# The short tile of tokens moved to the front, the last norm's shift added earlier, the last unit's sums turned on TensorE

## Chip, core and metric

The kernel runs on one core of one Trainium2 chip. The metric is the time on the device in microseconds (us), the median of several runs. A core has five engines with their own instruction streams: TensorE (PE: matrix products and transposes; its weight loads are PEld), VectorE (DVE), ScalarE (ACT), GpSimd (POOL) and SyncE (SP). SP, ACT and POOL also issue transfers (DMA).

## What is computed

800 tokens of 512 elements (8 sequences of 100) go through two layers, each an attention to a context of 8 x 722 rows and a mixture of 8 experts of which each token takes 2, with a residual after each of the four blocks:

```python
x = x + _L0_xattn_ref(_layernorm(x), ctx, ...)  # 16 heads of 32, causal: only the first 100 context rows count
x = x + _L0_ffn_ref(_layernorm(x), ...)         # 8 experts, 512 -> 2048 (GELU) -> 512, softmax weights of the top 2
x = x + _L1_xattn_ref(_layernorm(x), ctx, ...)  # 16 heads of 64; keys and values: own 100 tokens, 722 context rows
x = x + _L1_ffn_ref(_layernorm(x), ...)         # 8 experts, silu(gate) * up, 512 -> 1024 -> 512
```

The last block ends with a norm of its own output, before the residual:

```python
out = jnp.sum(rw[..., None] * sel, axis=2)      # the two experts' answers, weighted
mu, var = mean(out), mean((out - mu) ** 2)
out = (out - mu) * jax.lax.rsqrt(var + LN_EPS)
return out * ln_gamma + ln_beta
```

All is in float32.

## The kernel before

The 800 tokens lie in `x` as 7 tiles of up to 128 rows (one row to a partition): six of 128 and, last, one of 32 (`rows`). Everything that belongs to tokens and not to experts goes tile by tile.

**Layer 0.** After the norm, the columns and the attention, the output phase walks through the tiles (loop in the stage around L606 to L632): output product (L622), residual (L623), norm, transposes (`to_columns`, L153 to L166), router logits (`router_logits`, L173 to L178). Between them TensorE does context products (L425, L437) for attention 1 that are kept in memory.

**Routing.** `Route.group` takes a few tiles together, by the list `GROUPS`: for layer 0 tiles 0-2, 3-4 and 5-6. On VectorE it finds the two largest logits of each token (L227 to L241), marks them (`sel`, L245/L247), sums marks of earlier tiles (`before`, L249); TensorE counts the rows ahead (L252, L253, `ps_rank`); VectorE makes the place in the table (`row`, `pick`, `place`, `where`, L255 to L261); then POOL issues one indirect DMA for each tile and each of the two choices (L267), which scatters normed token rows into the table `sent`. When the last group is placed, `order` (L274 to L311) sorts the experts by their number of tokens; SP and POOL read the order into registers. `arrived` (L338 to L346) gathers an expert's rows from `sent` (L344, `xg`) and transposes them.

**Expert layers.** `work_off` goes through the 8 experts: `hidden0`/`hidden1`, then `products` (L348 to L365) and `returned` (L368 to L377), which writes rows to the table `answers`. `work_off` issues the next expert's `arrived` after the hidden products of the present one, and calls `midway`, if it has one, in the fifth. Layer 0 uses that for `fetch_context`. Weights come in 1 MB tiles on SP's queue (L58), eight buffers, each behind a one-element copy where it must wait (L56).

**Between the layers** each tile's two answers are gathered (`fetch`, L333), weighted and added to `x` (L723), normed and transposed (L724 to L728), and `bo` is added on POOL (L729).

**Attention 1** runs 64 units (8 sequences `b` times 8 pairs of heads `ic`) in a software pipeline: keys and scores of a unit (L778), the largest score (DVE, L782), the exponentials (ACT, L784, with their sums), and, one unit later, the transposes of the weights (L807 to L813), the values (L828) and the division by the sums. In sequences 0 and 1 (`EARLY`), whose keys were projected before, the reciprocal sums are copied wide by POOL (L792), transposed by TensorE (L822) and multiplied in at once (L832, L833). In the others they go to memory by SP (L795) and come back spread over partitions (L797), and the unit is multiplied by `over` a unit later (L835).

The list `due` puts three steps of each tile into the stream of units: `output` (L871 to L881: 16 matmuls L876 with the tile's rows as the stationary side, residual L879, norm) in unit `n`, `logits1` in `n + 1`, `sent_on` (the routing, by GROUPS 0-1, 2-3, 4, 5-6) in `n + 2`. `n` is two units after the last unit of the last sequence that the tile touches: 18, 26, 34, 50 and 58 for tiles 0 to 4. Tiles 5 and 6 both end in sequence 7, so theirs come after the last unit. The order of the instructions on each engine is set by a scheduler from the program.

**Expert layer 1 and the tail.** `gain` and `bias` (ln_gamma and ln_beta, spread over 128 partitions, 256 KB each) are loaded on ACT's queue at the stage's beginning (L929, L931). After the experts the two answers of each tile are gathered (L333), weighted into `acc` (L988, L990), normed, multiplied by `gain` (L998), added to `x` (L999) and stored (L1000). `x + bias` is written in the loop of the tail (L996), on POOL; the scheduler put these seven additions at the entry of the expert layer, where `bias` lands.

Of the kernel before, what the change touches and what calls it, by code (L numbers as in the profile page):

```python
# [8 lines left out]
F32 = mybir.dt.float32  # L9
AF = mybir.ActivationFunctionType  # L10
ALU = mybir.AluOpType
AX = mybir.AxisListType

P = 128
D = 512
DC = D // P
B, T, S = 8, 100, 722
NT = B * T
# [19 lines left out]
ROWS = NE * NT  # L38
GROUPS = ((0, 3), (3, 5), (5, NTILE)), ((0, 2), (2, 4), (4, 5), (5, NTILE))
LAST = NT - NT // P * P  # L40

# [25 lines left out]
def two_layers(ctx: ExitStack, tc: tile.TileContext, a: dict, out: bass.AP):  # L67
    nc = tc.nc
    x_in = a["x"].rearrange("b t d -> (b t) d")
    y_out = out.rearrange("b t d -> (b t) d")  # L70
    rows = [min(P, NT - i * P) for i in range(NTILE)]

# [28 lines left out]
    x = const.tile([P, NTILE, D], F32, name="x")  # L101
    nc.vector.memset(x[:, NTILE - 1, :], 0.0)
    for i0, i1 in ((0, 1), (1, 3), (3, NTILE - 1)):
        nc.scalar.dma_start(out=x[:, i0:i1, :], in_=x_in[i0 * P : i1 * P].rearrange("(i p) d -> p i d", p=P))
    nc.scalar.dma_start(out=x[:LAST, NTILE - 1, :], in_=x_in[NT - LAST :])

# [98 lines left out]
    class Route:  # L205


        def __init__(self, layer, psum, tag):
            self.layer, self.psum, self.tag = layer, psum, tag
            self.logits = routes.tile([P, NTILE, NE], F32, tag="logits", name=f"logits{layer}")  # L210
            nc.vector.memset(self.logits, 0.0)
            self.m = [routes.tile([P, NTILE], F32, tag=f"m{k}", name=f"m{k}_{layer}") for k in range(2)]
            self.where = [
                routes.tile([P, NTILE], mybir.dt.int32, tag=f"where{k}", name=f"where{k}_{layer}") for k in range(2)
            ]
            self.sel = routes.tile([P, NTILE, NE], F32, tag="sel", name=f"sel{layer}")
            nc.vector.memset(self.sel[:, NTILE - 1, :], 0.0)
            self.before = routes.tile([P, NTILE + 1, NE], F32, tag="before", name=f"before{layer}")
            nc.vector.memset(self.before[:, 0, :], 0.0)
# [16 lines left out]
        def group(self, i0, i1, xn):  # L236
# [5 lines left out]
            at2 = self.largest(other, self.m[1][:, i0:i1], 2)  # L242
            full = g if i1 < NTILE else g - 1
            if full:
                nc.vector.tensor_tensor(self.sel[:, i0 : i0 + full, :], at1[:, :full], at2[:, :full], ALU.add)  # L245
            if full < g:
                nc.vector.tensor_tensor(self.sel[:LAST, i1 - 1, :], at1[:LAST, full], at2[:LAST, full], ALU.add)  # L247
            for i in range(i0, i1):
# [221 lines left out]
    with tc.tile_pool(name="a0", bufs=1) as ap, tc.tile_pool(name="a0w", bufs=3) as aw, tc.tile_pool(  # L470
# [91 lines left out]
        for i in range(NTILE):  # L562
            xn = aw.tile([P, D], F32, tag="xn", name="xn0")
            scaled(xn, x[:, i, :], *factors(moments(x[:, i, :], "a0"), "a"))
            to_columns(xT, xn, i * P, rows[i], ps)
            nc.gpsimd.tensor_tensor(x[:, i, :], x[:, i, :], o_b, ALU.add)
# [41 lines left out]
        def logits0(i):  # L608
            xT = xTf[:, :, i * P : i * P + rows[i]]
            to_columns(xT, xl[:, i, :], 0, rows[i], ps)  # L610
            router_logits(route.logits, i, xT, wg0, bg0, ps, "av")
            for i0, i1 in GROUPS[0]:
                if i1 == i + 1:
                    route.group(i0, i1, lambda i: xl[:, i, :])

        for i in range(NTILE):
            w, t0 = rows[i], i * P
            if i % 4 == 0:
# [40 lines left out]
    with f0, tc.tile_pool(name="f0w", bufs=2) as fw, tc.tile_pool(  # L659
# [57 lines left out]
        for i in range(NTILE):  # L717
            w = rows[i]
            both = fp.tile([P, 2, D], F32, tag="nil", name="back0", bufs=2)
            for k, m in enumerate((m1, m2)):  # L720
                y = both[:, k]
                fetch(y, where, i, k)
                nc.vector.scalar_tensor_tensor(  # L723
                    x[:w, i, :], y[:w], m[:w, i : i + 1], x[:w, i, :], ALU.mult, ALU.add  # L724
                )
            xn = fp.tile([P, D], F32, tag="mv", name="xn1", bufs=2)
            scaled(xn, x[:, i, :], *factors(moments(x[:, i, :], "a1"), "b", twice=True))
            to_columns(xT1, xn, i * P, rows[i], ps, gamma1, beta1)  # L728
            nc.gpsimd.tensor_tensor(x[:, i, :], x[:, i, :], bo, ALU.add)  # L729
# [4 lines left out]
    with tc.tile_pool(name="a1", bufs=1) as ap, ExitStack() as later, tc.tile_pool(  # L734
# [25 lines left out]
        def values(b, ic, mT):  # L760
# [5 lines left out]
            return mv  # L766

        def weighed(b, ic, kT, mT):

# [19 lines left out]
            nc.vector.reciprocal(sums, sums)  # L789
            if b < len(EARLY):  # L790
                over = aw.tile([T, 2, H1], F32, tag="share", name="wide1", bufs=4)
                nc.gpsimd.tensor_copy(over, sums.unsqueeze(2).to_broadcast([T, 2, H1]))  # L792
                return prs, over
# [23 lines left out]
        def attended(b, ic, v, mv, prT, over):  # L817


            po = ps.tile([P, 2, T], F32, tag="tp", name="ps_av1")  # L820
            if b < len(EARLY):
                nc.tensor.transpose(po[:, 1, :], over.rearrange("t j d -> t (j d)"), ident[:T, :T])  # L822
# [6 lines left out]
            mine = qT[:, ic, b * T : (b + 1) * T]  # L829
            if b < len(EARLY):  # L830
                wide = small.tile([P, T], F32, tag="over", name="over2")
# [39 lines left out]
        def output(i):  # L871

            w, t0 = rows[i], i * P
            po = ps.tile([P, D], F32, tag="tp", name="ps_o1")
# [21 lines left out]
        for i in range(NTILE):  # L896
            n = min(t0 + T for t0 in range(0, NT, T) if t0 + T >= i * P + rows[i]) // T * IC + 2
            for k, step in enumerate((output, logits1, sent_on)):
# [19 lines left out]
        divide()  # L918
        attended(*before[:4], *turned(*before[4]))()
        for step, i in due[len(units)]:  # L920
# [4 lines left out]
    with tc.tile_pool(name="f1", bufs=1) as fp, tc.tile_pool(name="f1w", bufs=2) as fw, tc.tile_pool(  # L925
        name="f1p", bufs=2, space=bass.MemoryType.PSUM
    ) as ps:
        gain = fp.tile([P, D], F32, name="gain")
        nc.scalar.dma_start(out=gain, in_=a["ln_gamma"].partition_broadcast(P))  # L929
        bias = fp.tile([P, D], F32, name="bias")  # L930
        nc.scalar.dma_start(out=bias, in_=a["ln_beta"].partition_broadcast(P))  # L931
        where, more, (m1, m2) = route.where, route.more, route.m
# [27 lines left out]

        def work1(jobs, first=None):
            work_off(
                jobs, lambda e, r0, n: arrived(1, e, r0, n, fw, ps), hidden1,
                lambda e, n, h, wd: products(n, h, [wd(g) for g in range(NF // 4)], NF, fw, ps),
                lambda e, r0, n, yT: returned(1, e, r0, n, yT, fw, ps), first,
            )
# [6 lines left out]
            for e in range(NE)  # L973
        ], W_L1F)
        rest(
# [4 lines left out]
        acc = fp.tile([P, NTILE, D], F32, name="acc")  # L980
        nc.vector.memset(acc[:, NTILE - 1, :], 0.0)
        for i in range(NTILE):
# [11 lines left out]
        for i in range(NTILE):  # L994
            w = rows[i]
            nc.gpsimd.tensor_tensor(x[:, i, :], x[:, i, :], bias, ALU.add)  # L996
            scaled(acc[:, i, :], acc[:, i, :], *factors(moments(acc[:, i, :], "out"), "a"))
            nc.vector.tensor_tensor(acc[:, i, :], acc[:, i, :], gain, ALU.mult)  # L998
            nc.vector.tensor_tensor(x[:, i, :], x[:, i, :], acc[:, i, :], ALU.add)  # L999
            nc.sync.dma_start(out=y_out[i * P : i * P + w], in_=x[:w, i, :])  # L1000

# [69 lines left out]
```

## Time and profile before

| | us |
|---|---|
| median of 3 runs | 1884.36 |
| lowest and highest | 1884.31, 1885.33 |
| profiled execution, its own time | 1883.63 |
| its span, from the first to the last instruction | 1882.0 |
| PE busy in it | 1725.5 (92%) |
| DVE, ACT, POOL busy | 594.9, 479.7, 147.8 |

The stages in that execution, from the timeline: layer 0's output phase and routing lie about 179 to 231, its expert layer starts with the first transposes at 239.8, attention 1 with L414 at 684.4; the units' stream ends with the last scores near 1482, expert layer 1 starts at 1541.5 and the gathers of the tail at 1845.9.

In the lines of the timeline the columns are the start, the duration, the engine, the line, the operation, output and inputs with their shapes, the count, and in brackets the engine's idle time before it and what ended it. In lines of windows they are the stretch, its length, the busy time of PE, PEld, DVE, ACT and POOL with the number of instructions, the granted clock of TensorE as a share of full speed, the share of the DMA engines, and GB/s.

### The profile page before, as it was taken

To read this page: it belongs to the slowest core of one execution; us is meant where nothing else is said; L and a number is where in the kernel's file an instruction comes from. 1 tells how busy PE (TensorE), PEld (TensorE's weight loads), DVE (VectorE), ACT (ScalarE), POOL (GpSimd) and SP (SyncE) were. 2 spreads that over 40 slices of the span, in tenths; PEclk is the share of its full clock that TensorE was granted. 3 is DMA by queue.
4 is the path that set the end of the run, shared out by engine and by line. 5 is a ranking of instruction groups with operands and counts; after the bars stand their busy time and mean duration, and the time that the engine had idled before them with its cause. 6 is when DMAs were issued, how large, how long until landed. Compare 5 with 4: busy or idle time off the path is not lost. (4 is left out here: it accounts for less than half of the span.)

```text
span 1882.0 us, 26422 instructions
## 1 busy us (share of the span) xinstructions
PE 1725.5 (92%) x10414; PEld 1306.4 (69%) x10414; DVE 594.9 (32%) x1462; ACT 479.7 (25%) x1400; POOL 147.8 (8%) x237
## 2 busy tenths in 40 slices
PE   5999689999999879999999999999999849999990
PEld 2455479999999645666666666666666528999990
DVE  4464510011111220454344424444444331111115
ACT  2364211111111132333333323333333210010110
POOL 4010310000000220000000000000000030000003
PEclk9999889999999989999999999999999969999995
DMA  9901374465555361131020300202201145555523
GB/s 367 414 28 56 124 284 169 182 222 189 203 201 219 108 235 45 40 96 56 5 37 5 59 3 5 37 6 37 27 6 15 6 159 221 192 185 200 207 79 114
DMA packets 74657, 227.87 MB, mean 121 GB/s; under 512 B 26273, under 2 KB 37161, under 8 KB 58129
## 3 DMA queue, kind: packets, MB, share of 16 engines
q1 hardware_dynamic: 53020, 177.98, 27.7%
q0 software_dynamic: 9888, 30.06, 5.1%
q10 hardware_dynamic: 11604, 17.95, 3.2%
q8 instruction: 86, 1.41, 0.3%
q14 instruction: 59, 0.48, 0.1%
HBM read 177.12 MB, written 48.83 MB: 120 GB/s over the span
## 5 line engine op out<-in xcount | busy, mean ns | idle before, releaser
L425 PE MATMUL ps_m<-cb,w 128*128 128x361 f32 x944 | 315.7, 486 | 0.0
L356 PE MATMUL ps_y<-h,w 128*128 128x256 f32 (+7 forms) x1536 | 280.5, 344 | 0.0
L356 PEld LDWEIGHTS ps_y<-h,w 128*128 128x128 f32 x1536 | 268.6, 190 | 7.9
L425 PEld LDWEIGHTS ps_m<-cb,w 128*128 128x128 f32 x944 | 180.5, 196 | 110.5 <-issue 18.0
L680 PE MATMUL ps_h<-xgT,w 128*128 128x256 f32 (+7 forms) x1024 | 189.5, 346 | 0.0
L680 PEld LDWEIGHTS ps_h<-xgT,w 128*128 128x128 f32 x1024 | 180.8, 192 | 5.8
L784 ACT ACTIVATE pr<-ps_sc,m 100x822 f32<-100x822 f32 x128 | 119.9, 942 | 175.7 <-issue 89.9
L808 DVE COPY prT<-ps_ptA 128x500 f32<-128x500 f32 x128 | 82.1, 678 | 187.1 <-PE ps_ptA L807 187.1
L782 DVE TENSOR_REDUCE m<-ps_sc 100x1 f32<-100x822 f32 x128 | 123.8, 1009 | 46.7 <-PE ps_sc L778 46.7
L684 ACT ACTIVATE h<-ps_h,s_b 128x256 f32<-128x256 f32 (+7 forms) x128 | 56.1, 438 | 303.8 <-PE ps_h L680 303.8
L429 ACT COPY mT<-ps_m 128x361 f32<-128x361 f32 x128 | 58.8, 460 | 251.5 <-PE ps_m L425 226.1
L414 PE MATMUL ps_col<-xT,w 128*128 128x400 f32 x320 | 115.1, 518 | 1.3 <-ACT xT L166 1.3
L950 PE MATMUL ps_g<-xgT,w 128*128 128x256 f32 (+7 forms) x512 | 104.3, 347 | 0.0
L950 PE MATMUL ps_u<-xgT,w 128*128 128x256 f32 (+7 forms) x512 | 102.8, 344 | 0.0
L414 PEld LDWEIGHTS ps_col<-xT,w 128*128 128x128 f32 x320 | 61.9, 197 | 47.3 <-issue 4.2
L950 PEld LDWEIGHTS ps_g<-xgT,w 128*128 128x128 f32 x512 | 91.4, 192 | 3.0
L950 PEld LDWEIGHTS ps_u<-xgT,w 128*128 128x128 f32 x512 | 90.7, 190 | 2.7
L778 PE MATMUL ps_sc<-mT,qT 64*100 64x311 f32 (+1 forms) x512 | 91.3, 468 | 0.0
L828 PEld LDWEIGHTS ps_av<-prT,mv 128*64 128x64 f32 (+1 forms) x1536 | 67.9, 137 | 31.3 <-issue 28.9
L955 ACT ACTIVATE sg<-ps_g 128x256 f32<-128x256 f32 (+7 forms) x64 | 22.3, 348 | 238.8 <-PE ps_g L950 238.8
L828 PE MATMUL ps_av<-prT,mv 128*64 128x100 f32 (+1 forms) x1536 | 80.6, 253 | 0.0
L807 PEld LDWEIGHTS ps_ptA<-ident,pr 100*128 100x128 f32 x640 | 65.2, 141 | 20.7 <-issue 10.6
(242 smaller groups left out, 1799.6 us busy)
## 6 DMA issues: line engine op xcount, KB each, us to landing
w<-in_W SPq DMA_DIRECT2D x64, 1024.0 KB
w<-in_w_gate SPq DMA_DIRECT2D x16, 1024.0 KB
w<-in_w_up SPq DMA_DIRECT2D x16, 1024.0 KB
w<-in_w_down SPq DMA_DIRECT2D x16, 1024.0 KB
sent<-nil SPq DMA_DIRECT2D x25, 512.0 KB
answers<-nil SPq DMA_DIRECT2D x25, 512.0 KB
cb<-in_ctxT ACTq DMA_DIRECT2D x16, 722.0 KB
xg<-sent POOLq DMA_DIRECT2D x18, 256.0 KB
```

The costliest lines, as they stand in the source:

```text
L356: nc.tensor.matmul(py[:, k, :n], ws[f // 4][:, f % 4, dc * P : (dc + 1) * P], h[:, f, :n], start=f == 0, stop=f == nf - 1,)
L414: nc.tensor.matmul(ps[:, :HALF], w[c // 4][:, dc, (c % 4) * P : (c % 4 + 1) * P], xT[:, dc, cols], start=dc == 0, stop=dc == DC - 1,)
L425: nc.tensor.matmul(pm[:, : S // 2], w_m[ic // 4][:, dc, (ic % 4) * P : (ic % 4 + 1) * P], cb[h][:, dc, : S // 2], start=dc == 0, stop=dc = ...
L429: nc.scalar.copy(mT[:, h * (S // 2) : (h + 1) * (S // 2)], pm[:, : S // 2])
L680: nc.tensor.matmul(ph[:, :n], w[:, dc, j * P : (j + 1) * P], xg[:, dc, :n], start=dc == 0, stop=dc == DC - 1,)
L778: nc.tensor.matmul(sc[:, bank, c0:c1], qT[r, ic, q0 : q0 + T], keys_, start=True, stop=True)
L782: nc.vector.tensor_reduce(m, sc[:, :, :NKH], AX.XY, ALU.max, negate=True)
L784: nc.scalar.activation(pr.rearrange("p (a n) -> p a n", a=2), sc[:, :, :NKH], AF.Exp, bias=m, accum_out=sums[:, j : j + 1],)
L807: nc.tensor.transpose(pt[:, c, :], pr[:, T + c * P : T + (c + 1) * P], ident[:T, :T])
L808: nc.vector.tensor_copy(prT[:, : NSC - 1, :], pt)
L828: nc.tensor.matmul(po[r, 0, :], vj, prT[j][:w, c, :], start=c == 0, stop=c == NSC)
L950: nc.tensor.matmul(p_[:, :n], w_[:, dc, j * P : (j + 1) * P], xg[:, dc, :n], start=dc == 0, stop=dc == DC - 1,)
```

## The change

Three edits.

- The short tile becomes tile 0 (tokens 0 to 31); tiles 1 to 6 have 128 rows each and start at 32, 160, 288, 416, 544 and 672 (`starts`). `GROUPS` becomes 0-2, 3-5, 6 for layer 0 and 0-1, 2-3, 4-5, 6 for layer 1. By the rule of `due` the tiles' steps now start in units 10 (the short one), 18, 26, 42, 50 and 58, and only tile 6 is left for the end.
- `gain` and `bias` are loaded by `fetch_gains`, which `work_off` calls as `midway` in the fifth expert of layer 1: two one-element copies on POOL that wait for an `xg`, two DMAs on POOL's queue, and the seven additions `x + bias` on POOL. The additions of the tail's loop are gone. In POOL's order they stand after the gather of the sixth expert and before the answers of the third.
- The last unit (sequence 7, heads pair 7) turns its reciprocal sums like the early ones: POOL copies them wide, TensorE transposes them, ACT copies the result out of the accumulators, and VectorE multiplies. Its three transfers by SP are gone.

```diff
-GROUPS = ((0, 3), (3, 5), (5, NTILE)), ((0, 2), (2, 4), (4, 5), (5, NTILE))
-LAST = NT - NT // P * P
+GROUPS = ((0, 3), (3, 6), (6, NTILE)), ((0, 2), (2, 4), (4, 6), (6, NTILE))
+SHORT = NT - NT // P * P
...
-    rows = [min(P, NT - i * P) for i in range(NTILE)]
+    rows = [SHORT] + [P] * (NTILE - 1)
+    starts = [0] + list(range(SHORT, NT, P))
...
-    nc.vector.memset(x[:, NTILE - 1, :], 0.0)
-    for i0, i1 in ((0, 1), (1, 3), (3, NTILE - 1)):
-        nc.scalar.dma_start(out=x[:, i0:i1, :], in_=x_in[i0 * P : i1 * P].rearrange("(i p) d -> p i d", p=P))
-    nc.scalar.dma_start(out=x[:LAST, NTILE - 1, :], in_=x_in[NT - LAST :])
+    nc.vector.memset(x[:, 0, :], 0.0)
+    nc.scalar.dma_start(out=x[:SHORT, 0, :], in_=x_in[:SHORT])
+    for i0, i1 in ((1, 2), (2, 4), (4, NTILE)):
+        of_tiles = x_in[starts[i0] : starts[i0] + (i1 - i0) * P]
+        nc.scalar.dma_start(out=x[:, i0:i1, :], in_=of_tiles.rearrange("(i p) d -> p i d", p=P))
...
+        def turned_here(b, ic):
+
+            return b < len(EARLY) or (b, ic) == (B - 1, IC - 1)
...
-            if b < len(EARLY):
+            if turned_here(b, ic):
                 over = aw.tile([T, 2, H1], F32, tag="share", name="wide1", bufs=4)
                 nc.gpsimd.tensor_copy(over, sums.unsqueeze(2).to_broadcast([T, 2, H1]))
...
-            n = min(t0 + T for t0 in range(0, NT, T) if t0 + T >= i * P + rows[i]) // T * IC + 2
+            n = min(t0 + T for t0 in range(0, NT, T) if t0 + T >= starts[i] + rows[i]) // T * IC + 2
...
-        attended(*before[:4], *turned(*before[4]))()
+        attended(*before[:4], *turned(*before[4]))
...
-        gain = fp.tile([P, D], F32, name="gain")
-        nc.scalar.dma_start(out=gain, in_=a["ln_gamma"].partition_broadcast(P))
-        bias = fp.tile([P, D], F32, name="bias")
-        nc.scalar.dma_start(out=bias, in_=a["ln_beta"].partition_broadcast(P))
+        gain, bias = (fp.tile([P, D], F32, name=n) for n in ("gain", "bias"))
+
+        def fetch_gains(behind):
+
+            for t, n in ((gain, "ln_gamma"), (bias, "ln_beta")):
+                nc.gpsimd.tensor_copy(t[:1, :1], behind[:1, 0, :1])
+                nc.gpsimd.dma_start(out=t, in_=a[n].partition_broadcast(P))
+            for i in range(NTILE):
+                nc.gpsimd.tensor_tensor(x[:, i, :], x[:, i, :], bias, ALU.add)
...
         for i in range(NTILE):
             w = rows[i]
-            nc.gpsimd.tensor_tensor(x[:, i, :], x[:, i, :], bias, ALU.add)
             scaled(acc[:, i, :], acc[:, i, :], *factors(moments(acc[:, i, :], "out"), "a"))
```

The same turns of index (`starts[i]` for `i * P`, tile 0 for the last one) stand in the transposes, the clears of `sel` and `acc`, and the stores.

## The prediction

> **What bounds the kernel now.** I read the page first, then the waits of TensorE, then the timeline of the four places that the change touches: the routing of layer 0, the unit stream of attention 1, the entry of expert layer 1, and the tail.
>
> ```profile
> PE 1725.5 (92%) x10414; PEld 1306.4 (69%) x10414; DVE 594.9 (32%) x1462; ACT 479.7 (25%) x1400; POOL 147.8 (8%) x237
> PEclk9999889999999989999999999999999969999995
> ```
>
> TensorE is busy in 92% of the span, with its dips at the start, near 180 to 240, 660 to 690 and 1490 to 1545, and at the end. So TensorE work that is added inside a stream costs its full length, and other engines cost something only in the dips.
>
> ```profile
> PE ps_tp L157 <- DMA xg<-sent: 29.9, 3, 14.9
> PE ps_sc L778 <- ACT pr L784: 10.3, 10, 1.6
> PE ps_rank L252 <- DVE before L249: 10.2, 2, 9.1
> PE ps_o L876 <- DVE qT L835: 1.3, 1, 1.3
> ```
>
> The columns are total wait, times and longest. The first line is the two entries of the expert layers, the second is two short stalls in each of five output steps, the third is the routing at the end of attention 1, and the last is all that TensorE waits for the last unit's sums.
>
> The entry of expert layer 1, in the timeline (start, length, engine, line, and in brackets the idle time before it):
>
> ```profile
> 1503.59 8.64 PE L876 MATMUL ps_o<-w,qT 128*32 128x512 f32 x16
> 1503.69 0.17 DVE L178 COPY logits<-ps_lg 128x8 f32<-128x8 f32 x1 [3.81 <-PE ps_lg L173]
> 1516.43 8.57 POOL L996 TENSOR_TENSOR x<-x,bias 128x512 f32<-128x512 f32 x7 [59.14 <-DMA bias<-in_ln_beta]
> 1516.86 0.15 DVE L178 COPY logits<-ps_lg 32x8 f32<-32x8 f32 x1 [1.30 <-PE ps_lg L173]
> 1517.75 1.19 DVE L230 TENSOR_TENSOR at<-at,rank 128x16 f32<-128x16 f32 x1
> 1528.11 0.99 POOL L267 DMA_INDIRECT sent<-xnf,where  x1 [3.11 <-DVE place L260]
> 1531.84 0.86 POOL L267 DMA_INDIRECT sent<-xnf,where  x1 [0.30 <-issue]
> 1537.23 1.19 POOL L344 DMA_DIRECT2D xg<-sent  x2 [4.53 <-issue]
> ```
>
> Tile 5 is through at 1503.69; the short tile 6 repeats the chain until 1516.86; beside POOL's bias additions the small routing operations take up to 1.19 us; four scatters and the gather follow. All of it is serial.
>
> **The change part by part.** The sum is made against the profiled execution: span 1882.0, time 1883.63, which is 0.73 below the median of 1884.36.
>
> *Entry of expert layer 1.* (a) The short tile leaves: 1516.86 - 1503.69 = -13.17. In its place tile 6, now full, takes the chain that tile 5 had. (b) VectorE's clear of acc (0.48, at 1512.99) was in the short tile's chain and is now in the full one's: +0.48. (c) The bias additions leave: copy of the logits to first scatter was 1528.11 - 1516.86 = 11.25, and the same chain of a two-tile group in layer 0, without additions beside it, took 226.10 - 220.70 = 5.40; -5.85. (d) The group has one tile: two scatters instead of four, 1532.70 - 1528.11 = 4.59 against 1.28 + 0.97 = 2.25; -2.34. The full last scatter may land later than a 32-row one: taken +0.25, ends 0 and +1. (e) The last unit's sums: the round trip by DMA ended at 1495.46 and cost TensorE 1.29. In its place TensorE transposes wide1 (0.31 in the early units), but that transpose stands ahead of the unit's value products (1486.35), and it waits for the reciprocal (ends 1486.10) and POOL's copy (0.29, some 0.2 after the reciprocal in the early units): about +0.45 there. Net -0.84, ends 0 and -1.3. Sum: -21.5, range -20 to -23. The weights, issued at 1532.30 and needed at 1544.77, move with the chain. SP loses the three issues of the sums and ScalarE's queue the two of gain and bias (1512.30, 1512.69); neither queue had work behind them that the end waits for, so 0.
>
> *Unit stream.* The short tile is complete after unit 7, so its output, logits and routing fall due at unit 10 instead of after the last unit: one output step more among back-to-back TensorE work.
>
> ```profile
> 1027.78 0.66 PE L157 MATMUL ps_tp<-ident,xnf 128*128 128x128 f32 x4
> 1029.98 0.41 PE L778 MATMUL ps_sc<-kT,qT 64*100 64x100 f32 x2 [1.55 <-ACT pr L784]
> 1030.91 0.41 PE L778 MATMUL ps_sc<-kT,qT 64*100 64x100 f32 x2 [0.51 <-ACT pr L784]
> 1031.53 1.16 PE L173 MATMUL ps_lg<-p_w_router,xTf 128*128 128x8 f32 x8 [0.20 <-ACT xTf L159]
> ```
>
> Such a step makes its two units 16.86 and 16.09 long where plain ones take 10.0: +12.95 in four steps of five, +14.6 in the first. The products L876 are 16 whatever the rows (7.1 at 909.15); then 0.66 and 1.16, and 2.26 of stalls: 11.2. The rest, 1.75, is the clock:
>
> ```profile
> 1027.00:1032.00 5.00, 2.73 (x33) 2.04 (x29) 1.85 (x4) 3.86 (x7) 0.00 (x0) 1.00 0.02 0
> 1032.00:1037.00 5.00, 5.00 (x16) 3.21 (x16) 2.58 (x15) 0.16 (x1) 0.00 (x0) 0.66 0.00 0
> ```
>
> After the stretch with stalls (TensorE busy 2.73 of 5) the granted clock is 0.66 for 5 us, so 0.34 x 5 = 1.7 lost; the other steps show 0.50, 0.72, 0.70 and 0.66. The short tile: products 7.0, transposes 0.43, logits 0.42 (both as the short tile had at the end), stalls some 2.05 (in the new order the hoisted scores are longer and fill part of them), so 9.9, and 1.7 of clock: +11.6. Ends: 9.9 with no clock lost, 13.4 with twice as much, as in the first step. The Trainium skill, "TensorE: Matmul & The Clock Gate", Part 1, puts the drop after an idle window of about 3.4 us. By that rule stalls of 1.55 and 0.51 us would lose no clock, the step would cost 9.9 and the sum be 1.7 lower; five steps of five show the drop, so the row decides.
>
> *Routing of layer 0.* Groups (3,5) and (5,7) become (3,6) and (6,7). VectorE's order in the changed kernel has the row positions of group (3,6), then the copy of tile 6's logits, and only then where of group (3,6).
>
> ```profile
> 216.93 0.98 POOL L267 DMA_INDIRECT sent<-xl,where  x1 [9.08 <-DVE place L260]
> 219.08 0.17 DVE L178 COPY logits<-ps_lg 128x8 f32<-128x8 f32 x1 [2.09 <-PE ps_lg L177]
> 230.52 0.86 POOL L267 DMA_INDIRECT sent<-xl,where  x1 [0.30 <-issue]
> ```
>
> Before, scatters ran from 216.93 while the last two tiles were computed, and the last ended at 231.38. Now: tile 5's logits are copied about 216.95, the 24-wide chain to the rank product takes 3.78 (194.54 to 198.32), so 220.7; the logits of tile 6 stand behind it on TensorE and take 2.44 at the low clock (216.64 to 219.08), copy at about 223.65; 0.9 of pick, place and where and 0.4 to POOL: first scatter 225.0. Eight follow 1.28 apart, one 0.6 longer beside VectorE's L323: 225.0 + 7 x 1.28 + 0.97 + 0.6 = 235.5, and +0.4 as the last is full. Against 231.38: +4.5, ends +2.5 (logits at full clock, the chain tighter) and +6. The expert layer waits for nothing else here.
>
> *Hand-over to attention 1.* The last tile is full: transposes 1.08 against 0.60 (678.85, 682.51) and four ScalarE operations of 0.36: +0.7, ends 0 and +2.
>
> *Midway in expert layer 1.* Two one-element copies, two DMAs and seven additions on POOL, behind the sixth gather (second part issued 1658.44) and ahead of the answers at 1680.82. The landing of xg (3.8 at the entry, 1537.23 to 1541.03), copies and issues some 1.5, the bias landing 3.7 (1512.69 to 1516.43) and 7 x 1.26 = 8.8: 1676.2, 4.6 us early. VectorE's products of gate and up (0.39 every 2.97 us) may be held 1.26 each and still have 1.3 left. So 0, ends 0 and +2; without that cover the answers and the next gather would wait.
>
> *Tail.* The last gather and the last store are full: 0.4 each, the first gather is short: +0.5, ends 0 and +1. *Start:* TensorE waits for k_w until 18.7 whatever tile is first: 0, ends -0.5 and +1.
>
> Sum: -21.5 + 11.6 + 4.5 + 0.7 + 0.5 = -4.2, from 1884.36 to 1880.2.
>
> **The rivals.** 0.2% is 3.77 us, about what a measurement of this kernel can tell from no change; the bounds are 1880.6 and 1888.1.
>
> *A, the sum holds*, within 2.2 us: 1878.0 to 1882.4. *B, layer 0 pays less and the step loses no clock:* the scatters of group (3,6) start early enough that the queue is empty at the end (0 to +2.5), the step costs 9.9: 1874.0 to 1878. For it: scatters are short beside the chain. Against: the order on VectorE. *C, the gain is mostly eaten:* the step costs 13.4 as the first one did, layer 0 +6, hand-over +2, together 1.8 + 1.5 + 1.3 = 4.6 more, 1884.8; with one or two of them from 1882.4, at most 1886. For it: unit 10 lies where units take 7.0 and 7.8 instead of 10.0, with less TensorE work to hide ScalarE. *D, slower:* POOL's additions midway hold VectorE so that TensorE waits. The price is up to their own 8.8, so 1889.0. It decides once one product is held over 2.6 us, the room between two of them; the entry showed 1.29 at most, which speaks against it. *E, the sums' turn brings nothing*, since TensorE worked through most of the round trip: +0.84, 1881.0, inside A.
>
> **How the numbers follow.** A and E 0.55, B 0.20, C 0.17, D 0.08. A lies around 1880.2, so a little more than half of it is under 1880.6: faster 0.20 + 0.30 = 0.50, same 0.25 + 0.17 = 0.42, slower 0.08. The likeliest is 1880.2. For the range I leave out the far parts of B and D: 1875.0 to 1886.5.
>
> **What would show it.** Entry: logits copy to first scatter near 5.5 us, two scatters, TensorE's wait for xg shorter, and the first expert product some 21.5 us earlier against the last unit's scores. Stream: two units near 10 and 11 longer by 11.6 in all, a dip in the granted clock behind them, and two more stalls of L778's successor. Layer 0: first scatter of the second group near 225 and the last end near 236. Midway: seven additions ended before the answers, no new wait on TensorE. The prediction is wrong if the step at unit 10 stalls for more than 2.1 us, if the scatters of layer 0 end outside 234 to 237.5, or if TensorE waits in expert layer 1.

## The result: no difference that can be told

The changed kernel takes 1884.47 us (median of 12 executions, 1880.51 to 1888.23), the kernel before 1884.03 beside it (12 executions, 1881.47 to 1885.54). The ratio is 1.0001, with a 95% interval of 0.9992 to 1.0010: between 1.5 us faster and 1.9 us slower. The forecast was 1880.2 in a range of 1875.0 to 1886.5.

The page of the changed kernel's profiled execution (1880.57, span 1879.1) hardly differs in its sums:

```profile
span 1879.1 us, 26417 instructions
...
PE 1728.4 (92%) x10415; PEld 1309.5 (70%) x10415; DVE 587.2 (31%) x1462; ACT 482.3 (26%) x1402; POOL 150.7 (8%) x242
...
PEclk9999889999999989999999999999999979999995
```

The shares show nothing; the stages do. Below, each column is the time from one landmark of the timeline to the next: the first output product of layer 0 (L622 of the kernel before), the first expert product (L680), the first product of attention 1 (L414 after the experts), the first scores (L778), the end of the last scores, the first expert product of layer 1 (L950), the end of the last one (L356), and the end of the span.

| kernel | start | routing, layer 0 | experts 0, hand-over | columns | unit stream | entry, layer 1 | experts 1 | tail | span |
|---|---|---|---|---|---|---|---|---|---|
| before | 164.9 | 78.2 | 441.3 | 73.1 | 724.9 | 62.3 | 290.4 | 46.9 | 1882.0 |
| after | 164.8 | 83.9 | 438.1 | 74.0 | 739.7 | 38.3 | 290.9 | 49.3 | 1879.1 |
| difference | -0.1 | +5.7 | -3.2 | +0.9 | +14.8 | -24.0 | +0.5 | +2.4 | -3.0 |

The entry of expert layer 1 gained 24, and the stream, the routing and the tail took most of it back. The -3.2 can't be put down to the change: four other kernels without the short tile in front take 437.6, 438.1, 438.5 and 441.7 there.

The entry, in the timeline of the changed kernel:

```profile
1520.59 0.17 DVE L180 COPY logits<-ps_lg 128x8 f32<-128x8 f32 x1 [3.35 <-PE ps_lg L175]
...
1525.57 0.97 POOL L268 DMA_INDIRECT sent<-xnf,where  x1 [20.96 <-DVE place L261]
...
1526.85 0.97 POOL L268 DMA_INDIRECT sent<-xnf,where  x1 [0.31 <-DVE mine L308]
...
1530.86 1.17 POOL L345 DMA_DIRECT2D xg<-sent  x2 [3.04 <-issue]
...
1536.31 1.96 PE L159 MATMUL ps_tp<-ident,xg 128*128 128x128 f32 x8 [11.82 <-issue]
```

One logits copy instead of two, 4.98 from it to the first scatter instead of 11.25, two scatters instead of four, and the gather 3.04 behind the last one.

The routing of layer 0:

```profile
222.49 0.17 DVE L180 COPY logits<-ps_lg 128x8 f32<-128x8 f32 x1 [2.02 <-PE ps_lg L179]
...
223.53 0.98 POOL L268 DMA_INDIRECT sent<-xl,where  x1 [16.77 <-DVE at L232]
...
228.66 2.72 POOL L268 DMA_INDIRECT sent<-xl,where  x1 [0.30 <-issue]
...
234.24 0.97 POOL L268 DMA_INDIRECT sent<-xl,where  x1 [0.30 <-issue]
...
242.34 1.18 POOL L345 DMA_DIRECT2D xg<-sent  x2 [7.13 <-issue]
```

POOL stands still for 16.77 until tile 6's logits are copied, then issues eight scatters in a row, one of them at 2.72 beside VectorE, and waits 7.13 for the gather where it waited 5.39 in the kernel before:

```profile
236.78 1.18 POOL L344 DMA_DIRECT2D xg<-sent  x2 [5.39 <-issue]
```

The stream, as the time from the first value product of a unit (L828) to that of the next, where the two kernels differ by more than 0.5:

| units | before | after |
|---|---|---|
| 9, 10 | 7.00, 7.80 | 14.45, 12.69 |
| 26 | 16.09 | 17.66 |
| 33, 34 (a step before, none after) | 16.86, 16.09 | 9.99, 9.99 |
| 41, 42 (none before, a step after) | 9.99, 9.99 | 16.86, 16.09 |
| 50 | 16.09 | 17.39 |

The added step costs 7.45 + 4.89 = 12.3. The rest of the 14.8 is in the second units of other steps, which take 16.1 or 17.4 to 17.8.

### The profile page after: what moved, and what is told of

Same layout as the page of the kernel before. It is cut to its first block, busy times and chain, and to the rows that moved or that the text cites. A ratio compares the mean times of both kernels' runs of the same rounds, so it can differ in the third digit from the quotient of the medians.

```text
span 1879.1 us, 26417 instructions
## 1 busy us (share of the span) xinstructions
PE 1728.4 (92%) x10415; PEld 1309.5 (70%) x10415; DVE 587.2 (31%) x1462; ACT 482.3 (26%) x1402; POOL 150.7 (8%) x242
## 4 chain that ended last, share of the span: by engine, by line
PE 50%; issue 32%; DMA 11%; DVE 3%; ACT 2%; POOL 1%; POOLq 0%; ACTq 0%; another core or an unknown queue 0%; DVEq 0%
PE ps_m L426 16%; DMA answers<-y 8%; PE ps_col L415 7%; PE ps_sc L783 5%; PE ps_av L833 4%; PE ps_v L865 3%; PE ps_ptA L812 3%; PE ps_o L881 3%; PE ps_mv L438 2%; PE ps_v L517 1%; PE ps_o L623 1%; DMA xg<-sent 1%; DMA x<-in_x 1%; DMA back<-answers,where 1%; PE ps_lg L175 1%
## 5 line engine op out<-in xcount | busy, mean ns | idle before, releaser
L415 PEld LDWEIGHTS ps_col<-xT,w 128*128 128x128 f32 x320 | 60.9, 194 | 46.9 <-issue 2.3
```

The costliest lines, as they stand in the source:

```text
L415: nc.tensor.matmul(ps[:, :HALF], w[c // 4][:, dc, (c % 4) * P : (c % 4 + 1) * P], xT[:, dc, cols], start=dc == 0, stop=dc == DC - 1,)
```

## The experiments

Theory S: the time is the sum of these stages. Theory C: what else differs between executions is the clock behind pauses of TensorE.

### One part at a time

`tiles_only` is the changed kernel with the other two edits undone:

```diff
-        gain, bias = (fp.tile([P, D], F32, name=n) for n in ("gain", "bias"))
...
+        gain = fp.tile([P, D], F32, name="gain")
+        nc.scalar.dma_start(out=gain, in_=a["ln_gamma"].partition_broadcast(P))
...
-            if turned_here(b, ic):
+            if b < len(EARLY):
```

> The short tile first and the new groups, with gain and bias loaded and added as before and the last unit's sums by DMA. Theory S (the time is the sum of the stages as the profiled execution after the change shows them): routing of layer 0 +6.0, the added output step +12.4, the entry of expert layer 1 -13.2 for the tile and -2.3 for two scatters with the additions still beside the routing, tail +2.4, hand-over between -3 and 0: slower than before by 2 to 5 us. Rival R (the layer-0 delay is a matter of the moment and not of VectorE's order): layer 0 within 1.5 of before, and the time about 1 to 3 us faster.

Measured: 1887.93, ratio 1.0026 (1.0015 to 1.0037): 4.9 slower (2.8 to 7.0), as theory S expected. The routing of layer 0 takes 84.0 here too, 5.8 more than before, so rival R falls.

`gains_only` is the kernel before with `fetch_gains` as `midway` of layer 1, and without the other two edits:

```diff
-        ], W_L1F)
+        ], W_L1F, fetch_gains)
...
-            nc.gpsimd.tensor_tensor(x[:, i, :], x[:, i, :], bias, ALU.add)
             scaled(acc[:, i, :], acc[:, i, :], *factors(moments(acc[:, i, :], "out"), "a"))
```

> The kernel before with only gain, bias and the seven additions moved midway into expert layer 1. Theory S: the time from the last logits copy to the first scatter falls from 11.25 to about 5.6, everything else stays, -5.7 us. Rival D (the additions midway hold VectorE, TensorE waits): the same at the entry, but expert layer 1 takes up to 8.8 longer than the 290.4 from its first product to its last, so between -5.7 and +3.

Measured: 1876.33, ratio 0.9969 (0.9956 to 0.9982): 5.8 faster (3.4 to 8.3). In its timeline the last copy of logits and the first scatter of the entry:

```profile
1514.70 0.15 DVE L178 COPY logits<-ps_lg 32x8 f32<-32x8 f32 x1 [1.35 <-PE ps_lg L173]
...
1519.94 0.97 POOL L267 DMA_INDIRECT sent<-xnf,where  x1 [64.98 <-DVE place L260]
```

5.24 instead of 11.25, with the same group of two tiles: the additions alone had stretched it. Expert layer 1 takes 290.2, so rival D falls.

`sums_only` is the kernel before with the last unit's sums turned:

```diff
-            if b < len(EARLY):
+            if turned_here(b, ic):
...
-        attended(*before[:4], *turned(*before[4]))()
+        attended(*before[:4], *turned(*before[4]))
```

> The kernel before with only the last unit's sums turned on TensorE. Theory S: TensorE's wait of 1.29 before the last output products goes, its transpose costs some 0.4 ahead of the values, -0.9 us net, which the times can hardly tell. Rival E (the round trip was hidden in any case): 0, the output of tile 5 ends as late after the last scores as before (29.8).

Measured: 1883.06, ratio 1.0000 (0.9989 to 1.0012). In this profile nothing is gained, for a reason of its own; these are TensorE's products after its transpose of the wide sums:

```profile
1485.99 0.30 PE L826 MATMUL ps_av<-ident,wide 100*128 100x100 f32 x1
...
1486.54 1.95 PE L880 MATMUL ps_o<-w,qT 128*128 128x512 f32 x2
...
1488.42 1.97 PE L832 MATMUL ps_av<-prT,mv 128*64 128x100 f32 x21
...
1490.58 6.28 PE L880 MATMUL ps_o<-w,qT 128*128 128x512 f32 x14
```

The wait of 1.29 is gone, but the two groups at 1486.54 and 1488.42 took 1.95 and 1.97 instead of 1.12 and 1.16 before. That is the clock: 0.67 was granted from 1485 to 1490, where the kernel before had 1.00 in the same 5 us. It takes back 1.6. Between `tiles_only` and the changed kernel, whose clocks agree there, the step from the last scores to the addition to `x` goes from 14.34 to 13.33: the edit is worth 1.0, and the times can't tell it.

The three edits together give -5.8 + 4.9 + 0 = -0.9, and the changed kernel's interval, -1.5 to +1.9, holds that. So the parts add up within their intervals, and the tiles are the part that costs.

### The routing of layer 0

```diff
-GROUPS = ((0, 3), (3, 6), (6, NTILE)), ((0, 2), (2, 4), (4, 6), (6, NTILE))
+GROUPS = ((0, 3), (3, 5), (5, NTILE)), ((0, 2), (2, 4), (4, 6), (6, NTILE))
```

> The changed kernel with the groups of layer 0 as they were, tiles 0-2, 3-4 and 5-6. Theory S: the scatters of tiles 3 and 4 go out while the last two tiles are computed, four are left for the end, and the first expert product of layer 0 starts at 244 to 245 instead of 248.7: 4 to 5 us faster than the changed kernel. Rival R (the full last scatter and its landing are what layer 0 lost): it starts at 247 or later, 0 to 1.5 us faster than the changed kernel.

Measured: 1881.57, ratio to the kernel before 0.9993 (0.9982 to 1.0004), where the changed kernel has 1.0001: 1.5 faster by the times, within the intervals, and not the 4 to 5 of theory S. The first expert product starts at 245.6, between the two expectations; the stage takes 81.1, against 84.0 in the changed kernel and 78.2 in the kernel before.

```profile
219.95 0.97 POOL L268 DMA_INDIRECT sent<-xl,where  x1 [0.30 <-issue]
...
225.50 0.97 POOL L268 DMA_INDIRECT sent<-xl,where  x1 [4.58 <-DVE place L261]
...
226.77 2.58 POOL L268 DMA_INDIRECT sent<-xl,where  x1 [0.30 <-DVE experts L295]
...
230.93 0.97 POOL L268 DMA_INDIRECT sent<-xl,where  x1 [0.30 <-issue]
...
239.45 1.18 POOL L345 DMA_DIRECT2D xg<-sent  x2 [7.55 <-issue]
```

The scatters end at 231.90 as in the kernel before (231.38), so VectorE's order explains half of the loss. The other half is the wait of 7.55 behind them. Are the weights, which start meanwhile, in the way?

```diff
-                if s == 0:
+                if s == (NE - 1 if self.layer == 0 else 0):
                     load()
```

> The changed kernel with the first weights of layer 0's experts issued after SP has read the last of the eight entries of the experts' order instead of the first. Theory L (the gather of the first expert starts 1.7 later behind the last scatter, 7.1 instead of 5.4, because two full scatters drain beside the weights): the gather follows the last scatter after 5 to 6, and the first expert product starts 1 to 2 earlier, if the weights are there by then. Rival F (a full scatter simply lands later): still about 7 behind the last scatter, no gain.

Measured: 1884.54, ratio 1.0001 (0.9990 to 1.0011).

```profile
236.00 0.97 POOL L268 DMA_INDIRECT sent<-xl,where  x1 [0.30 <-issue]
...
236.22 15.50 SPq L58 DMA_DIRECT2D w<-in_W  x8
...
243.82 1.18 POOL L345 DMA_DIRECT2D xg<-sent  x2 [6.86 <-issue]
```

The weights' issues now start at 236.22, just after the last scatter's at 236.00 (in the changed kernel at 231.74, 2.5 ahead of it), and the gather still waits 6.86: the 5 to 6 that theory L expected is not there. The weights still load during the wait, so that they slow the landing is not excluded.

In layer 0 the eight kernels with full last scatters wait 6.9 to 7.6 there, the five with 32-row ones 5.0 to 5.4, about 2 less. The size of the last scatter alone does not explain it: at the entry of layer 1 the full ones (two scatters in the last group) are followed by the gather after 3.0 to 4.0, the 32-row ones (four) after 3.4 to 5.9. How many scatters are still under way, and what else loads then, differs between the two places, and no run separates these.

### The clock

> The changed kernel once more, unaltered, for a second profile and more times. Theory C (what differs between its executions, 1880.5 to 1888.2, is how long the clock stays low after the stalls of the output steps): the same units at the same lengths to 0.02, except those after an output step, which take either 16.1 or 17.2 to 17.8 (unit 10: 12.7 or 14.3), in another pattern than in the first profile; the entry and the routing differ by under 2. Rival M (the midway DMAs and additions collide differently from run to run): the stream repeats, and expert layer 1 differs by several us.

`after_again` is the changed kernel unaltered. Measured: 1884.69, ratio 0.9997 (0.9985 to 1.0008). The second profile repeats the stream to 0.1 in all, with the same pattern of long units, so theory C was wrong that this pattern changes from run to run. Elsewhere it does: `sums_only` has long second units at steps 18, 50 and 58, `gains_only` at 26 and 34, the kernel before at 18 alone, with the same code. The two profiles of the changed kernel differ in expert layer 1 (290.9 and 292.5). No wait differs there; what does is how soon the clock is back: the first 5 us were granted 0.62 and the next 1.00 in the one, 0.50 and 0.84 in the other. And over the first 12 executions of the changed kernel the time goes with the mean clock: the four at 0.958 took 1880.5 to 1882.1, the four at 0.954 took 1885.5 to 1888.2. That is consistent with C; it does not place each microsecond.

What makes the clock fall in an output step? `no_table` takes away ScalarE's two table loads, by leaving the root out of the norm ahead of the router:

```diff
+        if vector:
+            nc.vector.tensor_scalar(r, mv[:, 1:], EPS, None, ALU.add)
+            nc.vector.reciprocal(r, r)
...
-            scaled(xn, x[:, i, :], *factors(moments(x[:, i, :], "f1"), "a"))
+            scaled(xn, x[:, i, :], *factors(moments(x[:, i, :], "f1"), "a", vector=True))
```

> The changed kernel, with the root left out of the norm ahead of the router in layer 1 (the factor is 1 / (var + eps) on VectorE), so that ScalarE loads no table between the exponentials of a unit. Theory C: TensorE's stall of 1.55 in each output step falls under 0.5, the granted clock stays at 1 behind it, and the second unit of each of the six steps takes 12.5 to 14 instead of 16.1 to 17.8: 18 to 24 us faster than the changed kernel, 1861 to 1866, and the times spread less. Rival (the clock falls for other reasons than the stall): the steps lose only the stall, 6 x 1.3 = 8 us faster, and the granted clock still dips behind each.

Measured: 1869.95, ratio 0.9915 (0.9899 to 0.9932): 16 faster than the kernel before and, against `after_again` beside it, 14.7 faster than the changed kernel: between the 18 to 24 of theory C and the 8 of its rival. The second units take 14.8 in all five full steps, without long ones. But the dip is not gone, as the rival had said (windows: stretch, length, busy time of the five engines, granted clock, DMA share, GB/s):

```profile
1248.00:1253.00 5.00, 4.01 (x45) 2.66 (x42) 2.55 (x6) 2.58 (x6) 0.00 (x0) 1.00 0.02 3
1253.00:1258.00 5.00, 5.00 (x16) 3.19 (x16) 2.58 (x15) 0.02 (x1) 0.00 (x0) 0.66 0.02 0
```

TensorE was busy 4.01 of 5, its waits were 0.27, 0.51 and 0.20, and still 0.66 was granted afterwards. So either pauses of one microsecond in all are enough, or the small products count as rest. The waits alone do not decide it. In the short tile's step of the same run (first two lines) TensorE waited once, for 0.27, and the dip came; in an earlier stretch of the kernel before (last two lines) it waited 0.64, and none came:

```profile
856.50:861.50 5.00, 4.73 (x51) 3.28 (x52) 2.41 (x5) 2.27 (x6) 0.30 (x1) 1.00 0.29 74
861.50:866.50 5.00, 5.00 (x23) 3.24 (x22) 0.78 (x2) 0.84 (x4) 0.00 (x0) 0.66 0.00 0
...
802.10:807.10 5.00, 4.36 (x48) 2.75 (x44) 3.15 (x7) 2.38 (x7) 0.08 (x1) 1.00 0.99 328
807.10:812.10 5.00, 5.00 (x48) 3.27 (x48) 2.67 (x5) 2.48 (x7) 0.21 (x1) 1.00 0.37 118
```

`filled` puts work where TensorE waited:

```diff
             to_columns(xTf, sends[i], 0, rows[i], ps)
+            if i < NTILE - 1:
+                idle = ps.tile([P, D], F32, tag="tp", name="ps_idle")
+                for c in range(4):
+                    nc.tensor.matmul(idle, ident, w_o[0][:, c, :], start=True, stop=True)
```

> The changed kernel with four products of 512 columns (0.44 each) added on TensorE between the transposes and the logits of tiles 0 to 5 in layer 1; their result is not used. They stand where TensorE waited for ScalarE. Theory C1 (the clock falls because TensorE stands still in the output step): the granted clock stays at 1 behind the step or nearly so, and the two units of a step take 1 to 2 less although 1.8 of products came in, 5 to 10 us faster than the changed kernel. Rival C2 (the waits are too short for that; it is the small transposes and logits, which barely use the array, that count as rest): the dip of 0.66 stays and the step grows by 0 to 1.8, 0 to 10 us slower.

Measured: 1870.17, ratio 0.9926 (0.9909 to 0.9943): 13.9 faster than the kernel before, although TensorE has more to do in each of six steps.

```profile
1040.65 0.66 PE L159 MATMUL ps_tp<-ident,xnf 128*128 128x128 f32 x4
...
1041.15 3.60 PE L894 MATMUL ps_idle<-w,ident 128*128 128x512 f32 x8
...
1044.58 0.95 PE L175 MATMUL ps_lg<-p_w_router,xTf 128*128 128x8 f32 x8
...
1045.39 5.11 PE L426 MATMUL ps_m<-cb,w 128*128 128x361 f32 x16
```

Each added product is two instructions of 0.45, so 3.6 in all and not the 1.8 that the expectation counted. They fill the time in which the exponentials run, and the scheduler no longer moves the next unit's scores there. The windows of the same step:

```profile
1041.00:1046.00 5.00, 5.00 (x21) 2.94 (x20) 0.89 (x4) 3.34 (x7) 0.00 (x0) 1.00 0.02 0
1046.00:1051.00 5.00, 5.00 (x23) 3.26 (x22) 0.02 (x1) 0.92 (x2) 0.00 (x0) 1.00 0.03 3
```

and of the step at unit 18 in the kernel before:

```profile
926.00:931.00 5.00, 2.73 (x17) 2.15 (x15) 1.08 (x3) 3.70 (x7) 0.00 (x0) 0.90 0.02 0
931.00:936.00 5.00, 5.00 (x11) 3.14 (x11) 0.17 (x1) 0.00 (x0) 0.00 (x0) 0.50 0.00 0
```

The clock stays at 1.00, the second units take 14.65 instead of 16.1 to 17.7, and the stream 727.8 instead of 739.7. The small transposes and logits are all still there, so C2 falls as the only cause; and by the lines from `no_table`, the waits are not the only cause either. What is shown is that full work in place of the waits takes the dip away. In the full steps, waits of 2.26 give the short dip (second unit of 16.1) or the long one (17.4 to 17.8), 0.98 gives a dip without a long one, none gives none; how waits and small products count together stays open.

### What the short tile's step costs where it shares one

```diff
+            n = max(n, 2 * IC + 2)
             for k, step in enumerate((output, logits1, sent_on)):
```

with the groups of layer 0 as before:

> The changed kernel with the groups of layer 0 as before, and the short tile's output, logits and routing in the units of tile 1 (18, 19, 20) instead of 10, 11, 12. Theory S (of the 12.4 of the added step some 8 are products and transposes, the rest stalls and clock, paid once if two tiles share a step): units 9 and 10 are back at 7.0 and 7.8, units 17 and 18 grow by 8 to 9 in all, 3 to 4 us faster than with the groups of layer 0 alone, about 1878. Rival (the stall comes with each tile): the step costs 12 again, no difference.

Measured: 1879.47, ratio 0.9962 (0.9949 to 0.9974). Units 9 and 10 are back at 7.00 and 7.80; 17 and 18 take 23.84 and 19.12, 8.7 more than a step of one tile in the changed kernel (16.86 and 17.39). Of 12.3 some 8.7 are work and 3.6 pauses and clock, paid once if two tiles share them. Against `groups_back` the stream is 5.6 shorter in the profiles, and the ratio to the kernel before beside each falls from 0.9993 to 0.9962, which is 5.8.

### The gain at the entry without the price

> The kernel before (short tile last) with the gains midway and the sums turned, and after the last unit the output products of both tiles first, then the logits of both. Theory S: the short tile's products run while tile 5 is normed, so its logits are copied some 5 us after tile 5's instead of 13.2; the entry of expert layer 1 shortens by 5.8 for the additions, 1 for the sums and about 8 for the order, with nothing added to the stream and nothing changed in layer 0: 14 to 16 us faster than before, 1867 to 1870. Rival (VectorE and ScalarE, not TensorE, set the end of two tiles): 7 to 9 us faster.

```diff
-        for step, i in due[len(units)]:
+        for step, i in sorted(due[len(units)], key=lambda s: (output, logits1, sent_on).index(s[0])):
             step(i)
```

Measured: 1869.92, ratio 0.9922 (0.9905 to 0.9939): 14.7 faster than the kernel before, the short tile where it was, as theory S expected. The last two tiles in its timeline:

```profile
1499.64 0.68 DVE L883 TENSOR_TENSOR x<-ps_o,x 32x512 f32<-32x512 f32 x1 [4.04 <-PE ps_o L880]
...
1502.02 0.17 DVE L178 COPY logits<-ps_lg 128x8 f32<-128x8 f32 x1 [0.60 <-PE ps_lg L173]
...
1505.27 0.15 DVE L178 COPY logits<-ps_lg 32x8 f32<-32x8 f32 x1 [1.70 <-PE ps_lg L173]
...
1510.57 0.97 POOL L267 DMA_INDIRECT sent<-xnf,where  x1 [27.24 <-DVE place L260]
```

The second copy of logits follows the first by 3.25 instead of 13.17, since the short tile's products ran beside tile 5's norm. The entry takes 47.5 against 55.9 in `gains_only`, and the stream stays at 724.9. Some of the 8.4 belongs to the turned sums, which `gains_only` lacks: from the last scores to tile 5's addition it is 13.33 here and 14.88 there.

`together` adds the four unused products of `filled`, for tiles 0 to 4:

> The kernel before (short tile last, groups as before) with what paid: the gains midway, the sums turned, the output products of both last tiles first, and four unused products ahead of the logits of tiles 0 to 4. Theory C1 (the clock's dips go, and the stream shrinks by about 2 us in each of five steps, as with the added products in the changed kernel): the stream takes 714 to 716 instead of 724.9, the entry and the rest stay as with both outputs first: about 10 us under that kernel, 1858 to 1861. Rival (the gains do not add, since the added products delay the logits of the last groups): 1864 or more.

Measured: 1857.36, ratio 0.9849 (0.9833 to 0.9866): 28.5 faster than the kernel before (25.3 to 31.5), and faster than the changed kernel by about as much.

```profile
1025.00:1030.00 5.00, 5.00 (x22) 2.96 (x21) 1.12 (x5) 3.45 (x7) 0.00 (x0) 1.00 0.02 0
1030.00:1035.00 5.00, 5.00 (x23) 3.23 (x22) 2.30 (x14) 0.81 (x2) 0.00 (x0) 1.00 0.07 0
```

No dip here either; the stream takes 716.1.

The stages of all kernels, to read the above against:

| kernel | start | routing, layer 0 | experts 0, hand-over | columns | unit stream | entry, layer 1 | experts 1 | tail | span |
|---|---|---|---|---|---|---|---|---|---|
| after_again | 165.3 | 84.0 | 437.8 | 74.1 | 739.8 | 38.4 | 292.5 | 49.8 | 1881.7 |
| tiles_only | 164.3 | 84.0 | 437.5 | 74.3 | 740.0 | 44.0 | 291.4 | 49.2 | 1884.8 |
| gains_only | 163.8 | 77.3 | 438.5 | 74.3 | 726.3 | 55.9 | 290.2 | 48.1 | 1874.3 |
| sums_only | 165.2 | 78.0 | 437.6 | 73.4 | 727.7 | 63.7 | 290.2 | 47.9 | 1883.7 |
| groups_back | 164.5 | 81.1 | 437.2 | 73.2 | 742.1 | 38.6 | 290.9 | 49.3 | 1876.9 |
| weights_late | 166.5 | 84.1 | 438.4 | 74.4 | 740.0 | 38.8 | 292.3 | 48.6 | 1883.2 |
| no_table | 166.6 | 84.2 | 440.5 | 73.0 | 727.5 | 40.8 | 289.6 | 49.4 | 1871.6 |
| filled | 167.1 | 83.8 | 436.9 | 73.8 | 727.8 | 38.9 | 291.3 | 49.7 | 1869.3 |
| due18 | 166.9 | 81.2 | 438.2 | 74.4 | 736.5 | 38.6 | 292.5 | 49.3 | 1877.6 |
| both_outputs | 165.2 | 78.0 | 438.1 | 73.1 | 724.9 | 47.5 | 289.3 | 47.9 | 1864.1 |
| together | 164.3 | 77.1 | 441.7 | 74.6 | 716.1 | 47.4 | 289.4 | 48.7 | 1859.1 |

## Why the prediction was right, and by how little

The time lies in the range, 4.3 above the forecast. What was forecast, a gain of 0.22%, is not there: the interval ends at 0.08% faster. "Same" had a chance of 0.42 and "faster" 0.50. The terms, against the means over the kernels that share the code of each stage:

| term | predicted | measured | from |
|---|---|---|---|
| entry of expert layer 1 | -21.5 (-20 to -23) | -24.5 | 63.0 (before, sums_only) to 38.5 (five with all three edits) |
| unit stream | +11.6 (9.9 to 13.4) | +13.9 | 726.0 (four) to 739.9 (four); the step itself +12.3 |
| routing of layer 0 | +4.5 (2.5 to 6) | +6.3 | 77.7 (five) to 84.0 (six) |
| hand-over | +0.7 (0 to 2) | not told from 0 | 437.6 to 441.7 without, 436.9 to 440.5 with |
| midway | 0 (0 to 2) | 0 | 290.2 and 289.3 with it in the old order |
| experts 1 | no term | +1.5 | 289.9 (five in the old order) to 291.4 (eight in the new) |
| tail | +0.5 (0 to 1) | +1.4 | 47.9 (five) to 49.3 (eight) |

The forecast terms measure -2.9 together, and -1.4 with the stage that had no term; the times say +0.4, with -1.5 as the end of their interval, so the stages account for the result only at its edge. That the time lies in the range owes something to luck: the entry gained 3.0 more than the sum had, and the other stages cost 2.3, 1.8, 1.5 and 0.9 more. With the entry's forecast alone right it would have been about 1887.5, outside the range.

- **Entry.** The mechanism was right but for the last wait: the additions stretched the routing (5.24 and 4.98 without them), the sums are worth 1.0 (0.84 predicted). It was undersized by 3: the full tile's chain, from the last scores to the copy of its logits, took 19.99 instead of the 20.9 that the sum makes of it (21.24 - 0.84 + 0.48); the one-tile chain to the first scatter 4.98 instead of 5.40; and the gather followed the scatters after 3.04 instead of 4.53, where the sum had put 0.25 more. Most of that last 1.7 went again, since the first transposes came 5.45 behind the gather instead of 4.29; from them to the first product it was 2.63 instead of 3.25. That makes 2.5 in this pair of profiles; the rest of the 24.5 is that the sum went from 62.3, and `sums_only` has 63.7.
- **Stream.** The step is 12.3, and 11.6 was 0.7 short. The clock was right: 0.71 and 0.94 were granted in the two windows of 5 us behind the wait, 1.75 lost where 1.7 had been put. The wait was one of 1.39 instead of 2.05, and the products 9.2 instead of 7.85: the scores in these two units took 4.86 where the kernel before has 3.28. The further 1.6 is the clock in other steps, of which three instead of one had the long dip; the prediction had no term for this. The dip is there in each output step of both kernels, and also where only 0.98 of waits is left. The Trainium skill, "TensorE: Matmul & The Clock Gate", Part 1, puts the fall of the clock after an idle window of about 3.4 us. No output step has one, so the prediction was right to go by the row.
- **Routing.** The scatters were foreseen: first at 225.0, last end at 235.5; they were at 223.5 and 235.2. Two misses cancel in that: the start came 1.5 earlier, and the issue beside VectorE took 2.72, 1.75 longer than the others and not 0.6. The failed step is "+0.4 as the last is full": the gather waits 7.13 behind them and not 5.39, so 1.7.
- **Midway.** Additions end at 1670.9 and the answers go at 1675.4, 4.5 later, where 4.6 was predicted; TensorE does not wait there. Its one new wait, 0.68 just ahead of the first expert product, is in `tiles_only` too, without these additions, and not in `gains_only`, with them. The prediction had named a wait of TensorE in this layer as a sign against it; this one is small and comes with the tiles.

```profile
1653.07 0.54 POOL L345 DMA_DIRECT2D xg<-sent  x1 [2.49 <-issue]
...
1662.26 8.63 POOL L941 TENSOR_TENSOR x<-x,bias 128x512 f32<-128x512 f32 x7 [3.10 <-DMA bias<-in_ln_beta]
...
1675.43 0.56 POOL L378 DMA_DIRECT2D answers<-y  x1 [4.54 <-DVE y L377]
```

- **Experts 1.** The prediction put nothing here beyond the additions. `tiles_only` takes 291.4 without them, so the 1.5 is not theirs. Part of it is how soon the clock is back, as in the two profiles of the changed kernel (290.9 and 292.5); the rest was not separated.
- **Tail.** 0.8 was put for a full last gather and store, less 0.3 for the short first gather. From the end of the last gather's issue to the end of the span it is 18.2 to 18.9 in the five kernels of the old order and 19.3 to 19.8 in the eight of the new, so 1.1 instead of 0.8. The gathers themselves are not shorter: the last starts 17.2 to 17.9 after the first in the new order, and 17.3 to 18.3 in four of the five old ones.

Of the rivals, B (less for layer 0, no clock lost) and D (additions that hold TensorE) fell; C (the gain mostly eaten) is nearest to what happened, spread over three stages by 1 to 2 each; E is right for the times, which can't show a gain of 1.0.

A forecast 0.4 us past the bound of what can be told was half a coin toss, and the chances said so. What it missed in common is that four small costs were taken at or near nothing (the wait behind the last scatter in layer 0, the clock of other steps, expert layer 1, the tail), and all four came.

## What to carry to other kernels

A change of several parts should be costed and tried part by part: here one part paid 5.8, one cost 4.9 and one gave 1.0 in the trace, and together they looked like nothing. Before work is moved from a serial place into a busy stream, see whether it can run beside other work where it is; the same tile, left in place with its products ahead of the other tile's logits, brought the entry from 55.9 to 47.5 (with the turned sums, which are 1.0 to 1.5 of it) at no cost to the stream. Where TensorE waits briefly in a stream, look at the granted clock of the next 5 us: here waits of 2.26 cost 1.7 or more again, and unused products in their place were cheaper.

## What was not expected of the hardware

- Added, unused products made the kernel faster: 3.6 us of them in each of six steps took 11.9 off the stream, since the granted clock then stayed at 1.00; without them it is 0.66 over 5 us (as 3.4 us at the 0.50 of the long dip would give) or lower for longer.
- Waits of 0.27, 0.51 and 0.20 within about 3 us were enough for a dip to 0.66. One wait of 0.27 was enough in the short tile's step of the same run, and 0.64 elsewhere was not, so the products around a wait count too; how is open.
- In layer 0 the gather waits 6.9 to 7.6 behind full last scatters (128 rows) and 5.0 to 5.4 behind 32-row ones; at the entry of layer 1 it is 3.0 to 4.0 and 3.4 to 5.9. What sets the difference is open.
- Executions of one kernel spread by up to 9.6 us (the kernel before, 15 of them), and in 12 of the changed kernel the time followed the mean granted clock (0.954 to 0.958).
